# A routed mixture of experts on one core: from 74 weight-loading blocks and a final sum to three fixed blocks an expert and an adding scatter

## The chip, the core and the metric

The kernel runs on one core of a Trainium2 chip. The core has a matrix engine (TensorE, PE in the profile), a vector engine (VectorE, DVE), a scalar engine (ScalarE, ACT), a general engine (GpSimd, POOL) and a synchronisation engine (SyncE, SP) that issues most transfers; 16 DMA engines move data between the core's SBUF and HBM. Each engine works through its own queue in order. The metric is the device time of one execution in microseconds (us): the kernel before takes 3436.63 us, the median of three runs (3435.61 to 3440.5).

## What is computed

The input is a batch of 4 images of 32 x 32 tokens with 256 channels, so 4096 tokens. Layer 0 is a layernorm, a projection to 512, a depthwise 3 x 3 convolution, a state-space scan over 1024 steps with 64 states for each of 512 channels, a layernorm, a projection back, and a residual sum. Layer 1 is an attention with a 256 x 256 product a batch, and after it a mixture of 16 experts:

```
logits = x @ gate_w + gate_b;  probs = softmax(logits)
top_probs, top_idx = top_k(probs, 2);  top_probs /= sum(top_probs)
out[t] = sum over the token's two experts e of
         top_probs * ( silu(x[t] @ w1[e]) * (x[t] @ w2[e]) ) @ w3[e]
t = t + out                     # the residual sum is the kernel's output
```

The x of the experts is a layernorm of t. An expert's w1 and w2 are 256 x 512 and its w3 is 512 x 256, all float32: three tensors of 512 KB an expert. The reference multiplies every token by every expert; the kernel gathers for each expert only the tokens that chose it. Counting the reference's own choices for these inputs, the 16 experts get 411, 318, 424, 490, 591, 836, 278, 654, 596, 645, 718, 547, 389, 510, 475 and 310 of the 8192 (token, expert) pairs. In blocks of 128 rows that is 4, 3, 4, 4, 5, 7, 3, 6, 5, 6, 6, 5, 4, 4, 4 and 3: 73 blocks.

## The kernel before, in words

The scan takes most of the time and is not touched. The work around the change begins where the scan ends (2692 us into the profiled span) and is written out by hand, in the order in which each engine is to get it.

**Attention and routing.** `tbs[b]` is the part of `t_all` (128 x 32 x 256, the residual stream, 32 groups of 128 tokens) that belongs to batch b. The loop `for o in range(NB)` works on the attention of batch o while the routing of batch o-1 is drawn along in small steps (`steps = route(z)`, `on_with(steps, n)`). `expert_in` (L1475) writes the normalised rows to the HBM buffer `xd`. `route` finds the two experts of each token (`hot_all`, `first`), their weights (`wts`, L1552), each token's place among the tokens of its expert (L1558 to L1575), and from it its block (`within`) and its place in the block (`qb`), which `qh` (L1588) holds as a one-hot row of 128.

**The plan of the blocks.** After the last batch's routing, lines L1759 to L1825 count the blocks of each expert, give the blocks numbers (`first`, `end`), the expert of each (`eid`), and find by 64 matmuls over one-hot codes (L1795 to L1806) which (token, choice) stands in each row of each block: `src` (row of `xd` to read) and `dst` (row of `yd` to write).

**The blocks.** `blocks_of(0, NFULL)` with NFULL = 74 works on one block of 128 rows at a time, with transfers for the block four ahead (`AHEAD = 4`). `fetch_in` and `fetch_out` read the block's expert from `eid` on SP and load its w1, w2 (L1844) and w3 (L1857), and gather its rows from `xd` (POOL, L1850). `turn_rows` transposes the rows (L1868), `hidden` makes half of the hidden layer (L1881, L1886, L1887), `result` the product with w3 (L1893), and `put_result` copies it to `yb` (L1900, four buffers) and scatters its rows into `yd`, one row for each (token, choice) (POOL, L1901). All scatters write the tensor `yd`, so each waits for the landing of the scatter before it. Blocks 75 to 79 stand in a branch that is taken only if more than 74 are used; with 73 it is not.

**The final sum.** After the last scatter has landed, `yd` is read back in eight transfers of 1 MB (L1939), each row is multiplied by its weight and added to `t_all` (L1943, 64 instructions), and `t_all` is written to the output (L1947).

Of the kernel before, what the change touches and what calls it, by code (L numbers as in the profile page):

```python
# [8 lines left out]
F32 = mybir.dt.float32  # L9
BF16 = mybir.dt.bfloat16  # L10
# [23 lines left out]
def conv_ssm_attn_moe_kernel(ctx: ExitStack, tc: tile.TileContext, a: dict, out: bass.AP):  # L34
# [19 lines left out]
    NBLK = 2 * NB * L // BS + NE - 1  # L54
    assert 2 * NS == P
# [1112 lines left out]
    wts = l1.tile([P, 2, NTA], F32, name="wts")  # L1168

    t_all = l1.tile([P, NTA, C], F32, name="t_all")  # L1170
    xd = dram.tile([NB * L, C], F32, name="xd")

    yd = dram.tile([2 * NB * L + P, C], F32, name="yd")
# [4 lines left out]
    groups_f = l1.tile([P, NTA], F32, name="groups_f")  # L1178

    places = l1.tile([P, BS], BF16, name="places")  # L1180
    blocks_h = l1.tile([P, NBLK], BF16, name="blocks_h")

    groups = l1.tile([P, NTA], BF16, name="groups")
    part_pk = l1.tile([P, 2], F32, name="part_pk")
    spare = l1.tile([P, 1], F32, name="spare")
# [11 lines left out]
    def constants(first):  # L1197
# [6 lines left out]
        if first:  # L1204
# [4 lines left out]
            count(groups_f, NTA, 0)  # L1209
            count(part_pk, 2, 1, 1, 2)  # L1210
            count(spare, 1, 2 * NB * L + 1, 1, 1)
            count(block_p, 1, 0, 1, 1)
        else:
# [5 lines left out]
            nc.vector.tensor_copy(groups, groups_f)  # L1219

    with tc.tile_pool(name="wa", bufs=1) as wa, tc.tile_pool(name="att", bufs=1) as att, \
# [4 lines left out]
        tbs = [t_all[:, b * NT : (b + 1) * NT, :] for b in range(NB)]  # L1226
        for i in (0, HT):
            nc.sync.dma_start(out=tbs[0][:, i : i + HT, :], in_=rows(td, 0)[:, i : i + HT, :])
# [101 lines left out]
        def fourth(b, i):  # L1330
            on = batch[b]
            junk = sm.tile([P, C], F32, name="junk", bufs=1)
            nc.scalar.activation(
                junk, on["sq"][:, i, 0, :], AF.Square, accum_out=on["q4"][:, i : i + 1]
            )
# [124 lines left out]
        def expert_in(b, half):  # L1460
# [14 lines left out]
            nc.sync.dma_start(out=rows(xd, b)[:, lo:hi, :], in_=on["xe"][:, lo:hi, :])  # L1475
# [24 lines left out]
        def route(b):  # L1500
# [18 lines left out]
            first = sm.tile([P, NT], F32, name="first")  # L1519
            hot = [h[:, b * NT : (b + 1) * NT, :] for h in hots]  # L1520
            for k, top in enumerate((m1, m2)):
# [7 lines left out]
                nc.vector.tensor_reduce(first, cand, AX.X, ALU.min)  # L1529
                yield  # L1530
                nc.vector.tensor_tensor(hot[k], cand, over_last(first, NE), ALU.is_equal)
# [19 lines left out]
            for k, top in enumerate((m1, m2)):  # L1551
                nc.vector.tensor_tensor(  # L1552
                    wts[:, k, b * NT : (b + 1) * NT], top, both, ALU.mult
                )
# [30 lines left out]
            )  # L1585
            yield
            for k in range(2):
# [4 lines left out]
                yield  # L1592

# [32 lines left out]
        for o in range(NB):  # L1626
# [24 lines left out]
            turn_next(0)  # L1651
            v_out(o, 0)
# [70 lines left out]
            if n is not None:  # L1723
                fourth(n, NT - 1)
                k2(n, 1)
            out(o, 5)
# [5 lines left out]
            out(o, 7)  # L1732
            if n is None:
# [14 lines left out]
    eid = l1.tile([1, NBLK], I32, name="eid")  # L1748

    used_i = l1.tile([P, 1], I32, name="used_i")  # L1750
    NFULL = 2 * NB * L // BS + NE // 2 + 2
    src = l1.tile([P, NBLK], I32, name="src")
    dst = l1.tile([P, NBLK], I32, name="dst")
    wp = ctx.enter_context(tc.tile_pool(name="wp", bufs=6))
    with tc.tile_pool(name="rt", bufs=1) as rt, tc.tile_pool(name="rt2", bufs=3) as rt2, \
            tc.tile_pool(name="ps_r", bufs=1, space=PSUM) as ps_r:

        nbi = rt.tile([P, NE], I32, name="nbi")
        nc.vector.tensor_scalar(nbi, counts[-1], float(BS - 1), None, ALU.add)  # L1759
        nc.vector.tensor_single_scalar(nbi, nbi, BS.bit_length() - 1, ALU.arith_shift_right)  # L1760
        nb = rt.tile([P, NE], F32, name="nb")
        nc.vector.tensor_copy(nb, nbi)
        end = rt.tile([P, NE], F32, name="end")
        nc.vector.tensor_tensor_scan(end, every[:, :NE], nb, 0.0, ALU.mult, ALU.add)
        nc.vector.tensor_copy(used_i, end[:, NE - 1 :])
        first = rt.tile([P, NE], F32, name="first")
        nc.vector.tensor_tensor(first, end, nb, ALU.subtract)

        pick = rt.tile([P, 2 * NTA, NE], F32, name="pick")
        nc.vector.tensor_tensor(  # L1770
            pick, hot_all.rearrange("p k g e -> p (k g) e"), over_middle(first, 2 * NTA), ALU.mult
        )
        bf = rt.tile([P, 2, NTA], F32, name="bf")
        nc.vector.tensor_reduce(bf.rearrange("p k g -> p (k g)"), pick, AX.X, ALU.add)
        bh = rt.tile([P, 2, NTA], BF16, name="bh")
        nc.vector.tensor_tensor(bh, bf, within, ALU.add)

        done = rt.tile([P, NE], F32, name="done")
        nc.vector.tensor_scalar(done, end, block_p, None, ALU.is_le)
        ef = rt.tile([P, 1], F32, name="ef")  # L1780
        nc.vector.tensor_reduce(ef, done, AX.X, ALU.add)
        pe = ps_r.tile([1, P], F32, name="pe")
        nc.tensor.transpose(pe, ef, ident)
        nc.vector.tensor_scalar(eid, pe[:, :NBLK], float(NE - 1), None, ALU.min)

        pgp = ps_r.tile([P, 2, NBLK], F32, name="pgp")
        GC = NTA // 2
        n = 0  # L1790
        for k in range(2):
            for c in range(NTA // GC):
                gs = slice(c * GC, (c + 1) * GC)
                ih = rt2.tile([P, GC, NBLK], BF16, name="ih", bufs=2)
                nc.vector.tensor_tensor(  # L1795
# [185 lines left out]
```

## Time and profile before

| what | value |
|---|---|
| median of three runs | 3436.63 us |
| the profiled execution, its own time | 3446.1 us |
| its span | 3444.3 us |
| mean granted TensorE clock | 0.981 |
| blocks of experts: first transpose to last product | 2973.9 to 3401.7 us |
| in 2974 to 3402 us: PE busy, DMA share | 415.68 of 428 us, 0.91 |
| after the last product, to the end of the span | 42.6 us |
| weights loaded by the blocks | 222 transfers of 512 KB |

The page gives times of one execution, taken by the profiler. A row of the timeline is: start, duration, engine (an engine's name with q is its queue issuing a transfer), line, operation, output <- inputs, and in brackets how long the engine had been idle and what ended that. The view of waits says who waited for whom: total, times, longest. The view of stretches gives busy time of each engine in a stretch, the granted clock, the share of the 16 DMA engines that was busy, and the rate.

### The profile page before, as it was taken

The numbers are of one execution on the slowest core, as the hardware profiler recorded it, in microseconds if no ns is written. First come the engines' busy times: TensorE is split into PE (matmuls) and PEld (weight loads), VectorE is DVE, ScalarE is ACT, GpSimd is POOL, SyncE is SP. The second block draws the span as 40 slices with busy tenths as digits, with TensorE's granted clock in tenths as the row PEclk, the third lists the DMA queues.
The fourth block names the chain that finished last, engine by engine and source line by source line (L and its number), as shares of the span: only waits on it lengthen the run. The fifth ranks groups of instructions, "written<-read, shape, count | busy, mean of one in ns | idle before, by whom it ended". The sixth has DMA issues, their size and how long they took to land. (4 is left out here: it accounts for less than half of the span.)

```text
span 3444.3 us, 63146 instructions
## 1 busy us (share of the span) xinstructions
PE 3180.6 (92%) x23385; PEld 2757.0 (80%) x23385; DVE 2882.1 (84%) x3302; ACT 2714.7 (79%) x4611; POOL 2662.0 (77%) x1141
## 2 busy tenths in 40 slices
PE   7899999999999999999999999899999888699995
PEld 4588988988898988889988887688777566598894
DVE  4699999999999999999999999999999676422224
ACT  1699999999999999999999999999999444221110
POOL 0389998999999989999998999999899541133331
PEclk9999999999999999999999999999999999899997
DMA  3542223224232422243323225222122100799996
GB/s 103 151 68 64 67 68 67 71 70 67 66 76 67 75 69 71 65 57 84 72 68 71 67 65 75 57 62 65 57 65 65 53 19 25 243 327 310 317 313 227
DMA packets 442665, 348.59 MB, mean 101 GB/s; under 512 B 221153, under 2 KB 328929, under 8 KB 442354
## 3 DMA queue, kind: packets, MB, share of 16 engines
q1 hardware_dynamic: 422882, 320.74, 35.1%
q0 software_dynamic: 7104, 19.41, 1.7%
q10 hardware_dynamic: 12368, 4.37, 0.5%
q8 instruction: 187, 3.06, 0.4%
q14 instruction: 124, 1.02, 0.1%
HBM read 310.11 MB, written 33.78 MB: 100 GB/s over the span
## 5 line engine op out<-in xcount | busy, mean ns | idle before, releaser
L957 POOL TENSOR_TENSOR h<-h,cb_n 128x2048 f32<-128x2048 f32 x512 | 2146.4, 4200 | 134.5 <-DVE h L950 91.2
L924 ACT ACTIVATE da<-dt,l_conv_a_log_sb 128x512 f32<-128x512 f32 x2048 | 1435.4, 712 | 25.4 <-DVE h L950 24.4
L904 ACT ACTIVATE bx<-dtxT,proj 128x512 f32<-128x512 f32 x1748 | 1244.0, 712 | 29.6 <-DVE dtxT L596 17.0
L971 PE MATMUL y<-ident,h 128*128 128x128 f32 x8192 | 1238.0, 274 | 8.8 <-POOL h L957 5.8
L950 DVE TENSOR_TENSOR_SCAN h<-da,last,ps 128x512 f32<-128x512 f32 x1024 | 1218.0, 1269 | 6.8 <-PE ps L936 1.7
L950 DVE TENSOR_TENSOR_SCAN h<-da,ps 128x512 f32<-128x512 f32 x1024 | 1170.3, 1203 | 37.7 <-ACT da L924 9.7
L936 PE MATMUL ps<-ident,bx 128*128 128x128 f32 x6992 | 1118.0, 275 | 41.8 <-DVE h L950 28.7
L971 PEld LDWEIGHTS y<-ident,h 128*128 128x128 f32 x8192 | 980.4, 141 | 99.4 <-issue 20.3
L936 PEld LDWEIGHTS ps<-ident,bx 128*128 128x128 f32 x6992 | 819.1, 142 | 101.6 <-DVE h L950 80.1
L1887 DVE TENSOR_TENSOR hT<-s,p 128x256 f32<-128x256 f32 x148 | 62.4, 422 | 338.3 <-ACT s L1886 338.3
L1881 PE MATMUL p<-xT,w 128*128 128x128 f32 x2368 | 291.8, 277 | 0.5 <-ACT xT L1870 0.5
L1881 PEld LDWEIGHTS p<-xT,w 128*128 128x128 f32 x2368 | 285.0, 194 | 4.7 <-ACT xT L1870 0.9
L936 PE MATMUL ps<-ident,bxp 128*128 128x128 f32 x800 | 237.6, 297 | 53.6 <-DVE h L950 41.0
L1901 POOL DMA_INDIRECT yd<-yb,dst x74 | 73.0, 987 | 266.8 <-DMA yd<-yb,dst 161.0
L1886 ACT ACTIVATE s<-p 128x256 f32<-128x256 f32 x148 | 56.7, 383 | 275.0 <-PE p L1881 275.0
L409 PE MATMUL bg<-pad,dgc 128*128 128x256 f32 x864 | 258.2, 380 | 0.5 <-DMA dgc<-diags 0.5
L936 PEld LDWEIGHTS ps<-ident,bxp 128*128 128x128 f32 x800 | 112.0, 140 | 139.1 <-DVE h L950 84.2
L931 PE MATMUL ps<-dgb,dtxT 128*128 128x128 f32 x800 | 171.0, 296 | 22.0 <-DMA dgb<-diag_b 9.7
L915 POOL TENSOR_SCALAR bxp<-dtxT,proj 128x512 f32<-128x512 f32 x200 | 140.6, 703 | 60.5 <-DVE dtxT L596 60.5
L931 PEld LDWEIGHTS ps<-dgb,dtxT 128*128 128x128 f32 x800 | 120.8, 191 | 48.9 <-DVE h L950 35.2
L1893 PE MATMUL pf<-w,hT 128*128 128x256 f32 x592 | 152.5, 380 | 0.1
L1850 POOL DMA_INDIRECT xb<-xd,src x74 | 71.9, 972 | 96.5 <-DMA w<-in_L_ffn_w_dram 72.4
(310 smaller groups left out, 2435.5 us busy)
## 6 DMA issues: line engine op xcount, KB each, us to landing
cb_n<-cd SPq DMA_DIRECT2D x512, 256.0 KB, 3.3
w<-in_L_ffn_w_dram SPq DMA_DIRECT2D x222, 512.0 KB, 6.0
dgc<-diags SPq DMA_DIRECT2D x84, 192.0 KB, 3.1
diag_b<-zero SPq DMA_DIRECT2D x2, 4096.0 KB, 16.8
y<-yd SPq DMA_DIRECT2D x8, 1024.0 KB, 10.1
dgb<-diag_b SPq DMA_DIRECT2D x100, 64.0 KB, 3.1
last<-h SPq DMA_DIRECT2D x256, 2.0 KB, 3.0
xd<-xe SPq DMA_DIRECT2D x8, 512.0 KB, 2.9
```

The source lines that it names most:

```text
L409: nc.tensor.matmul(made["bg"].rearrange("p (h w) -> p h w", w=WW)[:, blk(c, deep), :], made["dgc", m * 3 + i][:, j, :], pads[m][:, at : at ...
L904: nc.scalar.activation(t, made["dtxT", u][:, j, :], AF.Copy, scale=made["proj", u][:, j, R + n : R + n + 1])
L915: nc.gpsimd.tensor_scalar(t, made["dtxT", u][:, 0, :], made["proj", u][:, 0, R + n : R + n + 1], 1.0, ALU.mult, ALU.mult,)
L924: nc.scalar.activation(t, made["dt", u][:, m, :], AF.Exp, scale=A[:, m, n : n + 1])
L931: nc.tensor.matmul(t[:, blk(j, P)], made["dtxT", steps[s][0]][:, j, blk(m, P)], made["dgb", s], start=True, stop=True,)
L936: nc.tensor.transpose(t[:, blk(j, P)], made["bx", s, j][:, blk(m, P)], ident)
L950: nc.vector.tensor_tensor_scan(h[:, m, 1:], made.pop(("da", s, m)), made.pop(("dbx", s, m)), 0.0 if seg == 0 else last[b][:, n, m : m + 1] ...
L957: nc.gpsimd.tensor_tensor(h[:, :, :BANK], h[:, :, 1:], over_middle(made["c", s], DK), ALU.mult)
L971: nc.tensor.matmul(made["y", u][j][:, blk(m, P)], made["h", s][:, m, blk(j, P)], ident, is_transpose=True, start=n == 0 and m == 0, stop=n ...
L1881: nc.tensor.matmul(p12[:, j, s, :], on[w, i][:, ck, blk(h + j, P)], on["xT", i][:, ck, :], start=(ck == 0), stop=(ck == CK - 1),)
L1893: nc.tensor.matmul(on["pf", i], on["hT", i][:, hk, :], on["w3", i][:, hk, :], start=(hk == 0), stop=(hk == HK - 1),)
L1901: nc.gpsimd.indirect_dma_start(yd[:, :], bass.IndirectOffsetOnAxis(dst[:, i : i + 1], 0), yb, None)
```

## The change

The blocks are planned in another way, the weighting and the sum move into the blocks, and the final sum goes.

- Every expert has three fixed blocks (FIX = 3, NFIX = 48); an expert's weights are loaded once for its three. The rows of the fixed blocks are found batch by batch inside `route` (a table `found`, 16 small matmuls a batch, DVE and ACT work on 48-wide codes), so after the last batch only `sources` (five small DVE operations) is left before the first gather.
- What an expert has beyond three blocks goes to "further" blocks, NFULL = 64 + 8 + 1 - 48 = 25 of them outside the branch, each with its own weights; they are mixed into the order from the 13th block on. Their plan (`more_places`, `more_rows`) runs in pieces beside the first blocks. The branch with 35 more blocks is taken if more than 25 are needed; the counts above need exactly 25.
- `xd` gets two more columns with the token's two weights (one small transfer a batch from SP), a row of `xd` is 1032 bytes, and 128 rows of zeros follow. `weigh` picks the weight of the row, and `put_result` multiplies by it where it copied before.
- The residual `tbs[o]` is written to the output right after batch o's attention, from the ACT queue, and the scatter adds into the output in HBM (`compute_op=ALU.add`). Unused rows of a block add zeros to tokens that do not occur in the block; a table of such tokens is made on POOL, PE and ACT during batches 2 and 3 (`nonmembers`, `count_them`, `place_them`, `list_them`).
- `ps_h` has three buffers in place of four; a bank goes to the plan. The weight buffers are three each for fixed and further blocks, in place of six.

```diff
-    NBLK = 2 * NB * L // BS + NE - 1
+    FIX = 3
+    NFIX = FIX * NE
+    NMORE = 2 * NB * L // BS - 2 * (FIX - 1)
+    NBLK = NFIX + NMORE
...
+        none = sm.tile([P, C + 2], F32, name="none_t", tag="junk", bufs=1)
+        nc.gpsimd.memset(none, 0.0)
+        nc.sync.dma_start(out=xd[NB * L :, :], in_=none)
         for i in (0, HT):
             nc.sync.dma_start(out=tbs[0][:, i : i + HT, :], in_=rows(td, 0)[:, i : i + HT, :])
...
+                nc.sync.dma_start(
+                    out=rows(xd, b)[:, :, C:], in_=wts[:, b * NT : (b + 1) * NT, :]
+                )
...
+            nc.vector.tensor_tensor(
+                ih, over_middle(blocks_h[:, :NFIX], 2 * NT),
+                over_last(at.rearrange("p k g -> p (k g)"), NFIX), ALU.is_equal,
+            )
+            yield
+            nc.vector.tensor_tensor(
+                code[:, :, 0, :], ih,
+                over_last(groups[:, b, :, :].rearrange("p k g -> p (k g)"), NFIX), ALU.mult,
+            )
+            for k in range(2):
+                nc.scalar.activation(
+                    code[:, blk(k, NT), 1, :], ih[:, blk(k, NT), :], AF.Copy,
+                    scale=part_pk[:, k : k + 1],
+                )
...
+            pf = ps_b.tile([P, 2, NFIX], F32, name="pf_r", tag="po")
+            for k in range(2):
+                for i in range(NT):
+                    nc.tensor.matmul(
+                        pf.rearrange("p s n -> p (s n)"), qh[:, k, b * NT + i, :],
+                        code[:, k * NT + i, :2, :].rearrange("p s n -> p (s n)"),
...
+                nc.vector.tensor_tensor(found, found, pf, ALU.add)
...
             out(o, 7)
+            nc.scalar.dma_start(out=rows(of, o), in_=tbs[o])
...
+        def fetch(key):
+
+            c, e = key
+            if c < NFIX:
+                if c < NE:
+                    load("", e, slice(e, e + 1))
+            else:
+                e = nc.sync.value_load(
+                    eid[0:1, c - NFIX : c - NFIX + 1], min_val=0, max_val=NE - 1
+                )
+                load("m", ("more", c), bass.ds(e, 1))
+            t = ffn.tile([P, C + 2], F32, name="xb", bufs=6)
             nc.gpsimd.indirect_dma_start(
-                t, None, xd[:, :], bass.IndirectOffsetOnAxis(src[:, i : i + 1], 0)
-            )
+                t, None, xd[:, :], bass.IndirectOffsetOnAxis(src[:, c : c + 1], 0)
+            )
...
+        def put_result(key):
             yb = ffn.tile([P, C], F32, name="yb", bufs=4)
-            nc.vector.tensor_copy(yb, on["pf", i])
+            nc.vector.tensor_scalar(yb, on["pf", key], on["wt", key], None, ALU.mult)
+            c = key[0]
             nc.gpsimd.indirect_dma_start(
-                yd[:, :], bass.IndirectOffsetOnAxis(dst[:, i : i + 1], 0), yb, None
-            )
+                of[:, :], bass.IndirectOffsetOnAxis(dst[:, c : c + 1], 0), yb, None,
+                compute_op=ALU.add,
+            )
...
+                if i < n:
+                    if i + AHEAD < n:
+                        fetch(todo[i + AHEAD])
+                    hidden(todo[i], 0)
+                next(beside, None)
+                if i > 0:
+                    result(todo[i - 1], 2)
+                    put_result(todo[i - 1])
+                if i + 1 < n:
+                    turn_rows(todo[i + 1])
+                if i < n:
+                    hidden(todo[i], 2)
+                    weigh(todo[i])
+                    result(todo[i], 0)
+                next(beside, None)
...
+        sources(0, NFIX, found[:, 0, :], found[:, 1, :])
+        fixed = [(s * NE + e, e) for e in range(NE) for s in range(FIX)]
+        more = [(NFIX + i, None) for i in range(NFULL)]
+        LEAD = 4 * FIX
+        todo, given = [], 0
+        for i, key in enumerate(fixed):
+            todo.append(key)
+            if i >= LEAD:
+                upto = NFULL * (i + 1 - LEAD) // (NFIX - LEAD)
+                todo += more[given:upto]
+                given = upto
+        blocks_of(todo, chain(spare_rows(), more_places(), more_rows(0, NFULL)))
+        used = nc.values_load(used_i[0:1, 0:1], min_val=1, max_val=NMORE + 1)
+        with tc.If(used > NFULL + 1):
...
-        for q in range(NTA // TPB):
-            y = fin.tile([P, TPB, 2, C], F32, name="y")
-            nc.sync.dma_start(out=y, in_=yds[q])
-            for j in range(TPB):
-                g = q * TPB + j
-                for k in range(2):
-                    nc.vector.scalar_tensor_tensor(
-                        t_all[:, g, :], y[:, j, k, :], wts[:, k, g : g + 1], t_all[:, g, :],
-                        ALU.mult, ALU.add,
                     )
-            nc.scalar.dma_start(out=ofs[q], in_=t_all[:, q * TPB : (q + 1) * TPB, :])
```

## The prediction

> **What bounds the kernel now.** I read the page first: after the scan all engines but PE fall, and DMA rises to 9 tenths.
>
> ```profile
> span 3444.3 us, 63146 instructions
> PE   7899999999999999999999999899999888699995
> DMA  3542223224232422243323225222122100799996
> ```
>
> Then the stretches of that stage: the blocks, a piece with weights still being loaded, the last blocks when all weights are there, and what follows the last product.
>
> ```profile
> 2974.00:3402.00 428.00, 415.68 (x3108) 391.48 (x3108) 93.69 (x222) 85.42 (x223) 139.02 (x142) 0.99 0.91 302
> 3376.00:3402.00 26.00, 25.66 (x191) 23.79 (x189) 5.99 (x15) 4.94 (x13) 8.79 (x9) 1.00 0.16 51
> 3402.00:3444.00 42.00, 0.00 (x0) 0.00 (x0) 25.87 (x65) 0.00 (x0) 0.97 (x1) 0.54 0.82 304
> ```
>
> PE is full in the blocks although DMA is nearly full as well. The timeline of PE gives the pace: from the transposes of one block to the next 5.53 us, with the weights' traffic and, the second pair, without it.
>
> ```profile
> 3370.08 0.41 PE L1868 MATMUL px<-ident,xb 128*128 128x128 f32 x2
> 3375.63 0.38 PE L1868 MATMUL px<-ident,xb 128*128 128x128 f32 x2
> 3381.15 0.38 PE L1868 MATMUL px<-ident,xb 128*128 128x128 f32 x2
> ```
>
> So traffic as such doesn't slow the products; reading the weights once gives nothing by itself. 74 x 5.53 = 409 of the 428 us; the rest is in the view of waits:
>
> ```profile
> POOL yd L1901 <- DMA yd<-yb,dst: 161.0, 44, 5.3
> PE px L1868 <- DMA xb<-xd,src: 20.1, 14, 8.6
> ```
>
> PE waits for gathered rows 20.1 us, of which 8.6 stand before the first block; 11.5 us are stalls between blocks. Their root is the first line: a scatter waits for the landing of the one before, and the gather for the block four ahead is queued behind it on POOL. The timeline of POOL shows this chain under full traffic and at the end, without it:
>
> ```profile
> 3003.32 1.00 POOL L1901 DMA_INDIRECT yd<-yb,dst  x1 [4.03 <-issue]
> 3004.62 0.97 POOL L1850 DMA_INDIRECT xb<-xd,src  x1 [0.30 <-issue]
> 3010.86 0.99 POOL L1901 DMA_INDIRECT yd<-yb,dst  x1 [5.27 <-DMA yd<-yb,dst]
> 3387.81 0.98 POOL L1901 DMA_INDIRECT yd<-yb,dst  x1 [2.23 <-DVE yb L1900]
> 3390.99 0.97 POOL L1901 DMA_INDIRECT yd<-yb,dst  x1 [2.20 <-DMA yd<-yb,dst]
> ```
>
> 7.5 us a link against 3.2 us. From 2985.07 to 3381.40 us POOL issued 68 scatters, on average 5.92 us apart: the chain is slower than PE's 5.53 and only four `yb` buffers and the four blocks of lead hide it. This margin decides the case. The chain that ended last starts at the last scatter and is the final sum alone: reads of `yd` 2.0%, its sums 1.9%, the scatter's landing 0.6%.
>
> **What the skill says.** The Trainium skill, DMA: Bandwidth & Descriptors, section Rules for kernel authors: an accumulating transfer reads its destination and writes it later, so another access of the same bytes must wait for its semaphore. The wait between scatters therefore stays, now for longer landings. The same page, Latency and other measured facts: HBM access takes 0.2 us on average and 2 us at high load. The Trainium skill, Collectives: The Full Stack, section The bandwidth ceiling: an add needs two source reads a chunk where a copy needs one, which halves the rate; about 31 GB/s an engine measured. The trace of before has no accumulating transfer; it agrees only that load stretches landings (3.2 to 7.5 us).
>
> **The change part by part**, against the profiled execution's 3446.1 us (span 3444.3 and 1.8 around it; it is 9.5 above the median, which I carry over by differences).
>
> *The end.* Removed: 42.6 us from the last product (3401.7) to 3444.3. Left: the copy 0.42 and the way to POOL 0.3, the scatter's issue and landing, 4.3 us from 3402.46 in the chain of waits; I take 5 for the add. 42.6 - 5.7: 37 us gained. Nothing hides it before, so all counts.
>
> *One block fewer,* 73 for 74: 5.5 us gained.
>
> *The plan before the first gather.* Before, the first gather is issued at 2967.66 and the scan over counts (L1558) starts at 2944.29. After, on DVE from there: scan and counts 0.65, three sums 0.97, two picks with reductions 1.44, six small ones to `at` 1.0, two 768-element codes 0.9 each (1264 elements take 1.47), `qh` 2 x 1.22, eight last matmuls 0.7 to 1 and `found` 0.25, five of `sources` 0.2 each: some 10.6, so 2954.9, 12.8 us earlier. The first weights depend on no table and are issued at the end of the gates' products (2935.5); six of them are there by about 2946 at the 310 GB/s of this stage. Before, the first gather took 6.2 us to the first transpose, among six experts' weights; after, nothing else runs, 3.8 (the least landing of a gather is 2.9). Together 15 us gained. The 8-byte writes of the weights stand ahead of the gather; 512 small rows of `last` land in 3.0 us, twice that is hidden in the 11 us from 2944.
>
> *The attention stage,* growth. (a) The zeros for `xd` stand ahead of the loads of `tbs` on SP: they wait for POOL's memset, and that for the scan's last product (to 2692.2), while the loads start at 2684.44 before. The first statistics come from 2693.04 to about 2699.5; ACT's root comes only at 2700.66 behind other work, so about 1.5 us remain. (b) A batch's codes: DVE 2.2, ACT 1.0, 16 matmuls of 1.3 to 2 us in PE's queue ahead of the gates; DVE has 5.9 us idle there (2898.7 to 2904.5), PE's part stays: 1.5 x 3. (c) 32 one-column matmuls for the table, 2 us in a stretch that DVE bounds: 1. (d) Four output writes on ACT, 0.42 us of issue each, one of them ahead of the last root: 1. POOL's 32 operations on the table lie in its idle time. Sum 8 us lost, from 3 to 15.
>
> *Beside the blocks.* 64 matmuls of 50 columns in PE's full queue, 0.06 to 0.08 each (158 columns: 2.68 us for 32), are 4.5; four places where PE waits for a DVE or ACT result made just before, some 0.6 each: 2.5. The extra DVE and ACT pieces (under 1 us a block) fit, as these engines are busy 94 and 85 of 428 us. The third `ps_h` buffer suffices: a block uses two, and the first is read 2.6 us before the third is written. 7 us lost.
>
> *Transfers.* 41 x 3 weights of 512 KB for 74 x 3: 64.5 MB for 116. SP's queue took 78% of the DMA engines for 115 MB, so 44% now; with the scatters' second read the share falls from 0.91 to about 0.65. A further block's buffer was freed three further blocks ago, over 7 blocks, against 4 of lead: no wait on weights.
>
> *The adding scatter.* Bounds of a link: as the plain one, 3.2 us unloaded and 5.9 loaded; or a gather and a scatter in series, 5.6 + 5.2 less one issue, 9.8 us loaded and 4.3 unloaded (2.9 + 2.4 - 1). My estimate from the skill's figures: 3.2, + 8 KB an engine at 31 GB/s 0.26, + one more HBM access 0.2 to 2: about 4.2 idle and 5.2 on average at a share of 0.65, under 5.53. Then the 11.5 us of stalls go and perhaps 3 remain: 8.5 gained. In the serial case 73 x 9.8 = 715 against 418 us (73 x 5.53 = 404, side work 7, start and last block 7): 297 lost.
>
> Sum: -37 - 5.5 - 15 + 8 + 7 - 8.5 = -51. 3446.1 - 51 = 3395 profiled, 3386 as median.
>
> **The rivals.**
>
> *The chain of adds is the bound (slower).* POOL's queue: scatter, landing, next scatter, with the gather for four blocks ahead behind it; once the four buffers are used up, `yb`, `pf` and PE follow the chain. The gain without stalls is 54, so it is lost when 73 links exceed 418 + 54 = 472 us: a mean link of 6.47 us decides. At 7.5 us the blocks take 548 us and the kernel 3437 - 54 + 130 = 3513. For it: links of 7.5 us with plain scatters under full traffic, a mean of 5.92 already. Against it: the traffic falls by a third, in the first 12 blocks to one expert in three blocks, and 3.2 us without traffic.
>
> *The chain costs a part.* A mean of 5.9 to 6.2 us: 13 to 35 us of stalls, 3396 to 3418. It needs nothing but the middle of the two bounds.
>
> *The branch is taken.* The counts need exactly 25 further blocks; one token more on expert 13 (510, three short of a fifth block) with two others, and 35 more blocks at 5.53 run: 3386 + 194 + some 10, 3590. The products are float32 as in the reference, so three such flips are very unlikely.
>
> *The change doesn't do what it says:* if the early plan's tables delay the attention by as much as they save, 15 us of the gain go: 3401.
>
> **How the numbers follow.** The main case (links under 5.6 us; 3366 to 3402) 0.57, with the last rival in it; a part of the gain lost to the chain (3402 to 3430) 0.17; within 0.2%, that is 7 us, about what a measurement here can tell from no change, 0.03; chain the bound, slower, 0.22; branch 0.01. Faster 0.74, same 0.03, slower 0.23. The range leaves out 0.06 below (attention without growth, no stalls, ends under 3366) and some 0.13 above: 3475 is a mean link of about 7 us. The main case's own range is 3366 to 3402.
>
> **What would show it.** The profile after should show the last adding scatter within 1.5 us of the last product and the span's end some 5 after; the first gather 4 to 6 us earlier than 2967.66 (12.8 less the growth); transposes 5.53 us apart; DMA share near 0.65 in the blocks; POOL's wait on the add's landing below 4 us a time, PE's wait for gathered rows under 10 us. The prediction is wrong if scatters stand over 6.5 us apart while PE waits for `xb` or `pf`; or if the first transposes come after 2974.

## The result, and the profile after

The changed kernel takes 3409.2 us (median of 4 runs, 3408.5 to 3409.6) against 3436.2 for the kernel before: a ratio of 0.9922, 95% interval 0.9907 to 0.9937. Faster by 27 us where 51 were forecast. In a second comparison (e9 below) its ratio was 0.9942 (0.9927 to 0.9958), so 20 to 27 us is what the change gives.

From the page of the changed kernel, its span and two of the rows that show it in 40 slices:

```profile
span 3407.1 us, 62616 instructions
PE   7899999999999999999999999989999898699997
DMA  3542223224232322243323224222112201377774
```

DMA has fallen from 9 tenths to 7 in the last slices, as forecast. The idle tail of PE has become shorter, not gone. The stretches of the same kernel (busy time and count of PE, PEld, DVE, ACT and POOL, then clock, DMA share and GB/s) cover the blocks and what follows the last product:

```profile
2961.50:3388.00 426.50, 413.29 (x3136) 389.65 (x3136) 127.70 (x432) 88.27 (x229) 182.69 (x142) 0.99 0.67 185
3388.00:3407.00 19.00, 0.00 (x0) 0.00 (x0) 0.41 (x1) 0.00 (x0) 3.18 (x3) 0.57 0.20 25
```

The blocks last 426.4 us from the first transpose to the last product, where 74 blocks before lasted 427.8: one block of 5.5 us is gone, and other losses have eaten most of it. Behind the last product (3387.89) stand 19.2 us. The second stretch counts three POOL instructions, but the first of them is the tail of a scatter issued at 3386.52; two scatters are still to be issued, where one was forecast. The view of waits over the same stage says what the scatters and the transposes waited for (total, times, longest):

```profile
POOL out_dram L1990 <- DMA out_dram<-yb,dst: 105.7, 35, 5.9
PE px L1944 <- DMA xb<-xd,src: 9.7, 9, 2.5
```

And the timeline shows single links of the chain, a link being the time from one scatter's issue to the next: one with quiet queues, one under a burst of weights (with VectorE's making of the data, `yb`, for its second scatter), and the last three scatters.

```profile
3028.53 1.59 POOL L1990 DMA_INDIRECT out_dram<-yb,dst  x1 [5.39 <-DVE dst L1893]
3033.16 1.59 POOL L1990 DMA_INDIRECT out_dram<-yb,dst  x1 [1.74 <-DMA out_dram<-yb,dst]
...
3185.04 0.48 DVE L1988 TENSOR_SCALAR yb<-pf,wt 128x256 f32<-128x256 f32 x1
3193.80 1.59 POOL L1990 DMA_INDIRECT out_dram<-yb,dst  x1 [3.16 <-DVE wt L1955]
3202.72 1.60 POOL L1990 DMA_INDIRECT out_dram<-yb,dst  x1 [6.04 <-DVE yb L1988]
...
3386.52 1.55 POOL L1990 DMA_INDIRECT out_dram<-yb,dst  x1 [3.19 <-issue]
3391.72 1.55 POOL L1990 DMA_INDIRECT out_dram<-yb,dst  x1 [3.64 <-DMA out_dram<-yb,dst]
3396.25 1.55 POOL L1990 DMA_INDIRECT out_dram<-yb,dst  x1 [2.99 <-issue]
```

An adding scatter takes POOL 1.59 us (a plain one 0.99), and the quiet link is 4.6 us (plain 3.2). Links beside weight loads run up to 9.7 us. From the first scatter (2974.47) to the 73rd (3396.25) the mean is 5.86 us, and a block of PE needs 5.52: the chain is slower than the products, all along. The name after the arrow needs care: a scatter waits both for its data and for the landing before it. For the scatter at 3202.72 the profile names `yb`, but this `yb` was ready at 3185.52, 17 us earlier. Matched in order, every scatter from the fifteenth on finds its data ready, by 1.5 to 18 us, and any gather ahead of it on POOL already issued, so it is the landing that they wait for.

The table is made from the timelines. Its first column runs from the start of VectorE's last pair of copies in the scan stage (`ysb`, at 2683.66 after and 2691.83 before) to the first transpose of gathered rows, the second on to the last product, the third to the span's end.

| us | scan's end to first transpose | blocks | end | mean link |
|---|---|---|---|---|
| before | 282.1 | 427.8 | 42.6 | 5.72 |
| after | 277.9 | 426.4 | 19.2 | 5.86 |
| after, again (e9) | 276.1 | 426.3 | 19.1 | 5.85 |

The 8.2 us between the two `ysb` copies lie ahead of everything that was changed; in the other runs of changed kernels this copy starts anywhere from 2688 to 2695, so I take them for chance. The other three differences, some 29 us, are the change.

### The profile page after: what moved, and what is told of

It is laid out like the page before. It is cut to its first block, busy times and chain, and to the rows that moved or that the text cites. A ratio compares the mean times of both kernels' runs of the same rounds, so it can differ in the third digit from the quotient of the medians.

```text
span 3407.1 us, 62616 instructions
## 1 busy us (share of the span) xinstructions
PE 3173.6 (93%) x23450; PEld 2753.0 (81%) x23450; DVE 2887.3 (85%) x3443; ACT 2715.8 (80%) x4623; POOL 2732.8 (80%) x1176
## 3 DMA queue, kind: packets, MB, share of 16 engines
q1 hardware_dynamic: 387586, 260.60, 29.6%
q0 software_dynamic: 14016, 19.22, 3.2%
## 5 line engine op out<-in xcount | busy, mean ns | idle before, releaser
L1990 POOL DMA_INDIRECT out_dram<-yb,dst x73 | 116.0, 1589 | 229.1 <-DMA out_dram<-yb,dst 105.7
L1972 ACT ACTIVATE s<-p 128x256 f32<-128x256 f32 x146 | 56.1, 384 | 266.0 <-PE p L1966 258.3
L1966 PE MATMUL p<-xT,w 128*128 128x128 f32 x1536 | 190.8, 278 | 0.6 <-ACT xT L1946 0.6
L1966 PEld LDWEIGHTS p<-xT,w 128*128 128x128 f32 x1536 | 185.7, 195 | 3.1 <-ACT xT L1946 1.0
L412 PEld LDWEIGHTS bg<-pad,dgc 128*128 128x128 f32 x864 | 130.5, 191 | 0.7 <-DMA dgc<-diags 0.7
```

The source lines that it names most:

```text
L412: nc.tensor.matmul(made["bg"].rearrange("p (h w) -> p h w", w=WW)[:, blk(c, deep), :], made["dgc", m * 3 + i][:, j, :], pads[m][:, at : at ...
L1966: nc.tensor.matmul(p12[:, j, s, :], w_of(w, key)[:, ck, blk(h + j, P)], on["xT", key][:, ck, :], start=(ck == 0), stop=(ck == CK - 1),)
L1990: nc.gpsimd.indirect_dma_start(of[:, :], bass.IndirectOffsetOnAxis(dst[:, c : c + 1], 0), yb, None, compute_op=ALU.add,)
```

## The experiments

**Theory A**: each adding scatter waits for the landing of the one before; with a mean link above the block's 5.52 us this chain sets the blocks' stalls (intervals between blocks exceed 5.52 us by 16 us in sum behind the first ten) and leaves two links open at the last product. **Theory B**: the stalls come from gathers and weights that crowd each other, and the chain costs only at the end.

### The addition, or the wait for it

```diff
             nc.gpsimd.indirect_dma_start(
                 of[:, :], bass.IndirectOffsetOnAxis(dst[:, c : c + 1], 0), yb, None,
-                compute_op=ALU.add,
             )
```

> Only the addition in the scatter is taken away: the 73 scatters overwrite rows of the output instead of adding to them, each still ordered behind the one before, so the output lacks the sums. Theory A (the chain of adds: a link of 5.86 us on the mean against 5.52 us a block makes both the stalls in the blocks, some 13 us, and the two links still open at the last product): the scatter costs GpSimd 0.99 us instead of 1.59, an idle link 3.2 us instead of 4.6, the mean link falls to the blocks' own period, the stalls fall to some 3 us, the stretch from the last product to the end from 19.2 to some 9 us, and the time from 3409 by about 20 to 3389 us (3384 to 3394). Theory B (the stalls come from gathers and weights that queue behind one another's packets, whatever the scatter does, and only the end hangs on the chain): stalls stay at 13 us, only the end falls, 3399 us (3396 to 3403).

```diff
+        turn = [0]
...
+            turn[0] += 1
             nc.gpsimd.indirect_dma_start(
-                of[:, :], bass.IndirectOffsetOnAxis(dst[:, c : c + 1], 0), yb, None,
+                (of if turn[0] % 2 else td)[:, :], bass.IndirectOffsetOnAxis(dst[:, c : c + 1], 0), yb, None,
                 compute_op=ALU.add,
```

> The adding scatters go in turn to the output and to a second buffer of the same shape, so each waits only for the one before the last; instructions, bytes and additions stay the same, and the two halves are not brought together, so the output lacks every second block. Theory A (it is the wait of each add for the landing of the one before): two chains of 37 links, each with 11 us a link to spare, are never late; stalls in the blocks 3 us, one scatter open at the last product, the end 19.2 to about 10 us, the time about 3390 us (3385 to 3394). Theory B (what costs is the additional work of an adding packet in the DMA engines, the wait being incidental): the bytes and packets are as before, so the blocks stay at 426 us and only part of the end goes, 3400 to 3409 us.

(`of` is the output, `td` the second buffer.) Measured: 0.9873 of the kernel before (0.9848 to 0.9897) without the addition (e1) and 0.9874 (0.9856 to 0.9892) with two targets (e2); on the 3436.2 us of the first comparison that would be 3393 us for both, 16 under the changed kernel. From the first transpose to the end they take 423.5 and 424.9 us, against 445.6 in the changed kernel. The stretches and the waits of the run with two targets:

```profile
2969.50:3382.50 413.00, 409.54 (x3135) 389.00 (x3136) 127.67 (x431) 88.10 (x229) 183.91 (x143) 0.99 0.68 192
3382.50:3394.00 11.50, 0.45 (x3) 0.05 (x1) 0.48 (x1) 0.00 (x0) 1.55 (x1) 0.62 0.18 26
```

```profile
POOL out_dram L1992 <- DVE yb L1989: 107.6, 37, 8.7
POOL td L1992 <- DVE yb L1989: 101.4, 36, 4.8
```

All scatters now wait for their data and none for a landing; the blocks fall from 426.4 to 413.4 us and the end to 11.5, with one POOL instruction in it. Since the 73 additions, their bytes and packets (14016 on the software queue, as in the changed kernel) and the weights are all as they were, it is the wait for the landing that costs 21 us here, and not the adding. Theory B's 3400 to 3409 fails: 13.0 us came out of the blocks. The plain scatter gains as much in another way: its links are shorter, though 14 of them still wait for a landing,

```profile
L1990 POOL DMA_INDIRECT out_dram<-yb,dst x73 | 72.2, 990 | 251.5 <-DVE yb L1988 165.7
q0 software_dynamic: 7008, 19.22, 1.7%
```

and the mean link of 5.57 us is the pace of the blocks. The packets of gathers and scatters fall from 14016 to 7008: 48 for each of the 146, so an adding scatter takes 144, three times as many. The Trainium skill, Collectives: The Full Stack, section The bandwidth ceiling, counts two source reads for an add and one for a copy; the direction agrees, the trace has more than that.

### More lead, or fewer weights

```diff
-        AHEAD = 4
+        AHEAD = 8
...
-            t = ffn.tile([P, C + 2], F32, name="xb", bufs=6)
+            t = ffn.tile([P, C + 2], F32, name="xb", bufs=10)
...
-            yb = ffn.tile([P, C], F32, name="yb", bufs=4)
+            yb = ffn.tile([P, C], F32, name="yb", bufs=8)
...
-        LEAD = 4 * FIX
+        LEAD = 4 * FIX + 4
```

> Nothing is left out: gathers are issued 8 blocks ahead instead of 4, with 10 buffers for rows and 8 for results instead of 6 and 4, and the first further block comes 4 fixed blocks later so that its rows are known. Theory A (the chain of adds, 72 links of 5.86 us): the products no longer wait, so the blocks take some 10 us less (416), but the chain ends when it did, and the end grows from 19 to about 29 us: 3409 us (3404 to 3413). Theory B (a shortage of fetched rows in the blocks): the blocks take 10 us less and the end stays: 3399 us (3395 to 3402).

```diff
             else:
-                e = nc.sync.value_load(
-                    eid[0:1, c - NFIX : c - NFIX + 1], min_val=0, max_val=NE - 1
-                )
-                load("m", ("more", c), bass.ds(e, 1))
+                pass
...
-            return weights[name, e if c < NFIX else ("more", c)]
+            return weights[name, e if c < NFIX else lent[c]]
...
```

> The 25 further blocks use the weights of the fixed block ahead of them instead of loading their own: 75 of the 123 weight transfers go (39 MB), the further blocks compute with another expert's weights, every scatter and wait stays. Theory A with the part of it that the link is 4.6 us when the queues are idle and is stretched to 6 to 9 us by bursts of weights: the mean link becomes shorter than the block, below 5.5 us, stalls 3 us, the end about 14 us (one link less), the time about 3393 us (3388 to 3398). If the link is long of itself (over 5.7 us without bursts), the time stays above 3404 us.

Measured: 0.9935 (0.9913 to 0.9957) with more lead (e3), which is 3414 us on the 3436.2, just above the range of theory A, and in that comparison 21 us more than with two targets. The stretches of that run:

```profile
2972.50:3386.50 414.00, 410.32 (x3136) 389.50 (x3136) 127.97 (x431) 88.09 (x229) 177.41 (x139) 0.99 0.70 190
3386.50:3416.00 29.50, 0.15 (x1) 0.00 (x0) 0.48 (x1) 0.00 (x0) 7.76 (x5) 0.54 0.20 25
```

The stalls are gone from the blocks, 414.0 us (413.4 with two targets), and most of them have come back behind the last product: 29.6 us, with five scatters in it, the first issued just as the last product ends. Blocks and end together are 443.6 us (445.6 in the changed kernel). Buffers only choose where the debt of the chain is paid.

With the 75 weight transfers of the further blocks left out (e4; `lent` names the expert of the fixed block ahead), 0.9869 (0.9851 to 0.9887), 426.3 us from the first transpose on. The stretch of its blocks and the waits of its scatters:

```profile
2970.50:3384.50 414.00, 410.19 (x3136) 389.50 (x3136) 127.82 (x431) 88.27 (x229) 184.47 (x143) 0.99 0.44 96
```

```profile
POOL out_dram L1987 <- DVE yb L1985: 152.7, 57, 9.1
POOL out_dram L1987 <- DMA out_dram<-yb,dst: 48.7, 13, 4.7
```

At a DMA share of 0.44 the mean link is 5.58 us, the blocks' own pace, and behind the first ten, long links (6.2 to 7) appear only once an expert. So the chain of adds costs what it does because of the weights that it shares the DMA engines with: of the mean link of 5.86 us, about 1.3 us stand over the quiet 4.6.

### The shape of the traffic

```diff
-                ("w1", CK, HID, "o (k p) h -> p (o k) h"),
+                ("w1", CK, HID, "o (p k) h -> p (o k) h"),
...
-                nc.tensor.transpose(px[:, ck, :], on["xb", key][:, blk(ck, P)], ident)
+                nc.tensor.transpose(px[:, ck, :], on["xb", key][:, ck : C : CK], ident)
...
-                            p12[:, j, s, :], w_of(w, key)[:, ck, blk(h + j, P)],
+                            p12[:, j, s, :], w_of(w, key)[:, ck, h + j : HID : HK],
```

> Nothing is left out: the weights are loaded with one run of 4 KB a partition (128 pieces a transfer) in place of two of 2 KB (first and second weight) or four of 1 KB (third); the products take the hidden units and features in the matching order, with strided operands. Theory A (the adds' links are stretched by bursts of weight packets): if pieces of 4 KB clear the DMA engines sooner, the DMA share in the blocks falls from 0.67, the mean link from 5.86 to about 5.55 us and the time by 10 to 16 us, to some 3395 us. If a burst takes what its bytes take, share, link and time stay (3405 to 3413 us). A strided operand that TensorE reads slower would show as a block longer than 5.52 us.

```diff
...
+            early = (("w1", AHEAD + 1), ("w2", AHEAD), ("w3", AHEAD - 1))
...
+                    for part, lead in early:
+                        if i + lead < n:
+                            weights_of(todo[i + lead], part)
...
```

> Nothing is left out: the three weight transfers of a block are issued five, four and three blocks ahead instead of all together four blocks ahead, so a burst is 0.5 MB instead of 1.5 MB; bytes as before. If a link is stretched by the bytes in flight beside it, the mean link stays near 5.86 us (fewer long ones, fewer at 4.6) and the time within 4 us of 3409. If it is the length of a burst that holds an add up, the long links (7 to 9 us) go and the time falls by 8 to 15 us.

Measured: 1.0657 (1.062 to 1.0694) with long rows (e6), a loss of 6.6%. Two groups by shape, first of the changed kernel, then of this run, tell why: the weight loads of the fixed blocks' products with w1 and w2, and those of the transposes (count, busy time, mean ns of one, idle time before them).

```profile
L1966 PEld LDWEIGHTS p<-xT,w 128*128 128x128 f32 x1332 | 159.6, 193 | 1.9
L1944 PEld LDWEIGHTS px<-ident,xb 128*128 128x128 f32 x132 | 18.0, 142 | 19.0 <-DMA xb<-xd,src 13.3
```

```profile
L1966 PEld LDWEIGHTS p<-xT,w 128*128 128x128 f32 x1413 | 336.4, 328 | 1.0
L1944 PEld LDWEIGHTS px<-ident,xb 128*128 128x128 f32 x136 | 26.6, 196 | 3.4 <-issue 0.2
```

TensorE loads a weight whose elements stand 16 bytes apart in 328 ns instead of 193, the block grows from 5.52 to 9.30 us, and what the longer pieces would have done for the chain can't be seen any more. One thing can: with 9.3 us a block no link is ever late, one scatter is open at the last product, and the end is 11.5 us, as with two targets. The Trainium skill, SBUF — State Buffer, section Door 1: The DMA port swizzle, has float32 reads free up to a step of 4 elements and paying when each access goes to a new 16-byte line; a step of 4, the edge of that figure, pays here, and so do the transposes' loads with a step of 2 (8 bytes), inside it: 196 ns instead of 142.

With the loads issued in three rounds (e7): 0.9945 (0.9932 to 0.9958), with a mean link of 5.98 us; links of 7.5 to 8.8 us remain. But the trace shows that the edit did not spread the traffic. What one round issues now belongs to three different blocks, and where these all load weights, three transfers still go together; two such rounds stand close in the issues on SP, here the first, fourth and last of six:

```profile
3087.61 0.38 SPq L1919 DMA_DIRECT2D w1m<-in_L_ffn_w_dram  x1
...
3090.73 0.38 SPq L1919 DMA_DIRECT2D w2m<-in_L_ffn_w_dram  x1
...
3092.45 0.38 SPq L1919 DMA_DIRECT2D w3m<-in_L_ffn_w_dram  x1
```

Six transfers start within 4.8 us, where in the changed kernel six took 6.6 us (3079.93 to 3086.5). So this run does not try shorter bursts, and whether they would help stays open.

### What closes the program

```diff
-        used = nc.values_load(used_i[0:1, 0:1], min_val=1, max_val=NMORE + 1)
-        with tc.If(used > NFULL + 1):
-            for _ in more_rows(NFULL, NMORE):
-                pass
-            blocks_of([(NFIX + i, None) for i in range(NFULL, NMORE)])
```

> Left out: the test at the end whether more than 73 blocks are needed, and the 24 further blocks behind it, which these inputs never run. The chain of adds is untouched, so theory A expects the links and the last landing where they were; if the engines' reading of the count and the jump fill the 6 us between that landing and the end, the end shrinks from 19.2 to some 15 us and the time by 3 to 5 us; if the 6 us are the program's own close, nothing changes (3407 to 3411 us).

Measured: 0.9906 (0.9868 to 0.9943), too wide to tell from the changed kernel (e8); the trace decides. In the timeline of POOL the last scatter of this run is

```profile
3398.27 1.55 POOL L1990 DMA_INDIRECT out_dram<-yb,dst  x1 [2.84 <-issue]
```

and the span ends at 3405.5: 7.2 us from the issue of the last scatter to the end, against 10.9 in the changed kernel and 10.7 with two targets. The test and the branch behind it (35 further blocks, not the 24 of the expectation) cost 3.6 us. Before, they stood ahead of the final sum, whose first read was issued at 3407.16, 0.4 us after the last landing, so at most this much of them showed. (This run's chain happened to be quicker as well, a mean of 5.77 us.) Reading the count earlier, below, doesn't save it; whether the jump or the code behind it costs was not tried.

### The last stage of the attention

Aligned at the first `pqk` product of the attention, the gates, routing scans and counts of the first three batches come within 2.7 us of where they came before, some later and some earlier. The growth behind that product lies in the last batch: its gates are 9.2 us late (8.5 in e9). The timeline there, in the changed kernel:

```profile
2923.04 0.59 ACT L1275 COPY xeT<-ps_t 128x512 f32<-128x512 f32 x1 [0.21 <-PE ps_t L1274]
...
2929.91 0.82 PE L1634 MATMUL pf_r<-code,qh 128*128 128x96 bf16 x8 [5.92 <-DVE qh L1626]
2931.04 0.82 PE L1634 MATMUL pf_r<-code,qh 128*128 128x96 bf16 x8 [0.31 <-DVE qh L1626]
2931.79 2.66 PE L1502 MATMUL pgT<-xeT,l_ffn_gate_w_sb 128*16 128x512 f32 x4
```

PE stands 5.9 us at the products of the batch *before* (L1634), because VectorE is still making their one-hot rows, and the gate products of the last batch, whose `xeT` is ready at 2923.63, queue behind it. Three attempts took that wait away by issuing the old batch's products and the table later.

```diff
-            if o == 3:
-                list_them()
...
                 expert_in(o, 1)
-                on_with(steps, 40)
         gates(o, 0)
         turn_e(o, 1)
         gates(o, 1)
+        on_with(steps, 40)
         turn_g(o)
+        list_them()
```

> Nothing is left out: in the last of the four attention stages the rest of the plan of the batch before (its codes, its 16 products and the sum) is issued behind the gate products of the last batch instead of ahead of them, and the table of spare rows behind the turn of the last gates instead of between two output products. If the growth of the attention part (the last gates come 9.2 us later than before, the first three stages within 2 us of before) is TensorE's queue standing at those products until VectorE has made their one-hot rows, and 2.6 us of it the table's copy waiting on ScalarE, the last gates come 7 to 9 us earlier and the whole takes 5 to 9 us less, about 3402 us against 3409. If VectorE's additional codes themselves are the cause (5 us of work in that stage), the time falls by under 2 us.

The kernel as changed ran again (e9) beside the second attempt (e10) and a third kernel (e11), which is the second attempt and also reads the count in mid-course (`midway` calls `values_load` at half of `todo`). In e10 and e11 the zero row is written behind the loads of the tokens as well, an edit that the next cut leaves out.

> The changed kernel once more, to stand beside the next two on this chip. Its ratio to before should be 0.992 (0.9905 to 0.994); first transpose of rows to the end 445 us (442 to 450), as the links differ by 0.05 us or so between executions.

```diff
-            if o == 3:
-                list_them()
...
                 expert_in(o, 1)
-                on_with(steps, 40)
+                on_with(steps, 2)
         gates(o, 0)
         turn_e(o, 1)
+        on_with(steps, 3)
         gates(o, 1)
         turn_g(o)
-        steps = route(o)
+        earlier, steps = steps, route(o)
+        on_with(steps, 1)
+        on_with(earlier, 40)
+        list_them()
         on_with(steps, 40)
```

> Nothing is left out. Against the changed kernel: in the last attention stage the codes and one-hot rows of the batch before keep their place on VectorE, but their 16 products and the sum go behind the first step of the last routing, and the table of spare rows behind that; and the zero row is written behind the loads of the tokens instead of ahead of them. If the 9.2 us of attention growth are TensorE's queue (6.6 us at the products, 2.6 us at the table), the last gates come 8 to 9 us earlier than in the changed kernel and, unlike the first attempt, the routing scan and the first gather too: 7 to 9 us less to the first transpose; with the zero row another 0 to 1 us. Time 7 to 10 us under the changed kernel's. If only 3 to 4 us arrive at the first gather, a second wait has taken the first one's place.

> As the run before, and the engines read the count of further blocks in the middle of the blocks, not behind them; the test and the jump stay at the end. If the 3.5 us that the branch costs are the reading of the count, the end shrinks from 19 to about 16 us and the time by 3 us; if they are the jump, the end stays, and the reading costs up to 1 us in the middle.

The last attempt moves `on_with(steps, 3)` behind `gates(o, 1)`, and `earlier` and `list_them()` behind the eighth and tenth step of the last routing; the zero row is back in its place.

> Nothing is left out. The second attempt at the last stage again, with what its trace showed mended: the codes' ScalarE copies behind both gate copies, the 16 products and the sum of the batch before behind the counting products of the last routing, the table's copy behind that. If these were the waits that took the place of the first ones, the last gates, the routing scan and the first gather all come 8 us earlier than in the changed kernel, the first transpose of rows 270 us after the scan's last copy against 277.9 and 276.1 (changed kernel, two executions) and 282.1 before; the blocks and the end stay at 445 us (442 to 450). Time about 8 us, or 0.23%, under the changed kernel's: a ratio to before of 0.9905 (0.989 to 0.992).

Measured, in us from the start of the scan's last pair of copies (`ysb`):

| | last gate copy | routing scan | first gather | first transpose | blocks + end | ratio to before |
|---|---|---|---|---|---|---|
| before | 243.7 | 252.5 | 275.8 | 282.1 | 470.4 | 1 |
| after | 254.0 | 262.8 | 274.7 | 277.9 | 445.6 | 0.9922 |
| e9, after again | 252.3 | 261.1 | 273.0 | 276.1 | 445.3 | 0.9942 (0.9927 to 0.9958) |
| e5 | 247.3 | 259.2 | 271.2 | 274.4 | 449.6 | 0.9912 (0.9883 to 0.9942) |
| e10 | 247.4 | 258.3 | 270.2 | 273.4 | 447.1 | 0.9912 (0.9895 to 0.9928) |
| e11 | 246.3 | 257.2 | 269.1 | 272.2 | 449.7 | 0.9923 (0.9905 to 0.9941) |
| e12 | 247.0 | 256.7 | 268.6 | 274.3 | 444.2 | 0.9900 (0.9883 to 0.9916) |

The cause is shown: with the products out of PE's way the last gates come 5 to 8 us earlier each time. That VectorE's work itself was the cause is refuted, as all of it is still there. But each time a part of the gain was taken by the next wait: of the 7 to 9 us expected at the first transpose, 2 to 6 arrived. In e5 the old products and their sum stood ahead of the turn of the last gates, in e10 and e11 ahead of the second step of the softmax: from the last gate copy to the routing scan it is 11.9 us in e5 and 10.9 in the other two, where the changed kernel has 8.8. In e12 it is 9.7, the gather comes 4.4 to 6.1 us earlier, and then the weights are late. The issues of the first weights on SP, first of the changed kernel, then of e12:

```profile
2937.67 2.99 SPq L1917 DMA_DIRECT2D w<-in_L_ffn_w_dram  x6
2945.74 0.37 SPq L1569 DMA_DIRECT2D xd<-wts  x1
2946.14 1.61 SPq L1917 DMA_DIRECT2D w<-in_L_ffn_w_dram  x3
```

```profile
2949.91 0.36 SPq L1569 DMA_DIRECT2D xd<-wts  x1
2951.53 6.14 SPq L1921 DMA_DIRECT2D w<-in_L_ffn_w_dram  x9
```

In e12 all nine first transfers start at 2951.5, directly behind the table's copy at 2951.43. The weights now share the DMA engines with the first gathers, and gather to transpose takes 5.7 us instead of 3.1. That the weights wait for the one-hot ranks' memory (`at_rank`, whose last reader is the table) is inferred from these times and was not tried by itself. The zero row behind the loads (e10, e11) brings the first statistics 4 to 5 us earlier but the first `pqk` product by nothing clear (16.3 and 18.0 us from the copy against 17.9 to 19.2 elsewhere). The count read early leaves the end at 19.6 us, with 10.7 us behind the last scatter's issue as elsewhere: it is not the reading that costs.

e12 has the lowest ratio of the kernels that leave nothing out. In one comparison with the changed kernel (3419.8 us) stood e10 (3411.3) and e11 (3415.6); the intervals of the ratios of e10 and e9 just meet, those of e11 and e9 overlap, and the spread of the chain itself (blocks and end 444 to 450 us in kernels that do the same there) is as large as the gain. A small improvement of 2 to 8 us (the first transpose comes 2 to 6 us earlier; e10 takes 8.5 us less) is likely, not settled.

## Why the prediction was off by half the gain

The time, 3409 us, lies above the main case (3366 to 3402) and in the one that was given a chance of 0.17, a part of the gain lost to the chain. The two sums, prediction against the traces:

| step | forecast | after (e9) |
|---|---|---|
| plan before the first gather, gather to transpose | -15 | -14.5 (-14.5) |
| attention stage | +8 | +10.3 (+8.6) |
| blocks: one fewer, side work, stalls | -7 | -1.5 (-1.6) |
| end | -37 | -23.4 (-23.5) |
| sum | -51 | -29.0 (-31.0) |

The same sum for the run with two targets is 276.8 + 413.4 + 11.5 against 752.5 before: -50.8. Without the chain of waits the forecast total would have stood, but by luck: the end gains 31.1 us there and not 37, the blocks 14.4 and not 7, and the misses cancel.

**The adding scatter** is the step that failed, and the stalls and the end with it. It was put at 4.2 us quiet and 5.2 on average, under 5.53; it measured 4.6 and 5.86. Of the quiet part the estimate left out that POOL itself issues an add 0.6 us longer (1.59 against 0.99). For the load it allowed 1.0 us on top, without a working; 1.3 was measured, at a share that came as forecast (0.67). The quiet 4.6 with the 1.0 allowed would already have been 5.6, slower than the products. The mechanism named in the second rival, the chain costs a part (5.9 to 6.2 us, 3396 to 3418), is what happened, with a link at its lower edge. The forecast's own sign, POOL's wait on a landing below 4 us a time, already says so: the longest is 5.9.

**Stalls.** Forecast: 11.5 fall to 3. Measured by intervals between blocks: 16.1 before, 16.3 behind the first ten after. That 3 was right for blocks that the chain does not hold: behind the first ten the excess is 3.2 us with two targets, and 3.2 with the plain scatter, which still waits for its landings. The gain from less traffic was thus real, and given back whole to the longer links of the add.

**The end** left 5.7 us, and 19.2 came. From the last product to the last scatter's issue it is 8.4 us instead of 0.7 (two targets: 0.8), 7.6 us for the two open links. From that issue to the end it is 10.9 instead of 5: 3.6 for the test that closes the program (e8), which the step left out: it removed the whole of the old end, ahead of which the test had stood hidden behind the last landing; 1.7 for the addition itself (10.7 with two targets, 9.0 with the plain scatter); the remaining 0.6 was not attributed.

**The attention stage** was right in size and wrong in place. Of its 10.3 us (8.6 in e9), 1.1 (0.1) lie ahead of the first `pqk` product, where (a) had 1.5. From there to the last normalisation of the last batch (L1484) it is 2.6 (1.0), where (c) and (d), the table and the output writes, had 2; the table's copy came 2.6 us after its products in both, behind four other instructions on ScalarE, and PE waited 0.7 us for it. The rest, 6.6 (7.6), is the wait for the products in PE's queue. (b) charged them 1.5 us in each of three stages; they cost nothing there, and all of it in the last stage, where no other work was left to put ahead of them.

**Right**: the plan (from the last routing scan to the first gather 11.4 us less, forecast 12.8), the first gather (3.1 us to the transpose, forecast 3.8), the DMA share, a pace of 5.52 us, no branch taken; the first ten blocks, with most of the side work beside them, stalled 3.8 us in all, where 7 were forecast. The break-even of 6.47 us a link was not tested: at 5.86 the chain lost two fifths of the gain (21 of 51 us), more than the 10 us that the same working (73 links against 418 us) gives.

## What to carry to other kernels

When scatters must add into one buffer, the wait for each landing makes a serial chain; compare its *mean* link under the stage's own traffic, not the quiet one, with the period of the engine that is to be the bound, and if it is longer, a second target (here without the sum of the two, which would cost something) or less traffic helps, while more buffers only move the loss to the end. When a tail is removed, list what used to hide in it, a test or a branch, and charge it to what is last now. In a queue that issues in order, a product moved earlier must find its operands ready: what stood idle harmlessly beside other work costs its full wait in the stage that has nothing left to put ahead.

## What the runs showed that was not expected

- An accumulating indirect scatter of 128 rows of 1 KB costs GpSimd 1.59 us against 0.99, takes three times the packets of the plain one, and 4.6 against 3.2 us a quiet link, and up to 9.9 us (e9) beside weights, at 185 GB/s in the stage.
- A float32 weight load with a step of 16 bytes takes 328 ns against 193, and that of a transpose with a step of 8 bytes 196 against 142.
- Executions of one chain differ: blocks and end took 444 to 450 us in kernels that are the same there, and 436 without the closing test, of which the test explains 3.6. What sets this is open.
